# The beginning of a fused attention and feed-forward block: decay rows read back later, four x loads at once, values one chunk behind

## The chip, the core and the metric

The kernel runs on one core of one Trainium2 chip. The metric is the device time of one launch in microseconds (us), taken as the median of several runs.

## The reference

All tensors are float32. x has 8 batches of T = 1024 rows with V = 512 columns, D is 128, and there are three decays.

```python
xn = (x - mean(x)) / sqrt(var(x) + 1e-5)            # over the 512 columns
q, gate = xn @ Wq, softmax(xn @ Wg)                 # gate: 3 values a row
for i in range(3):
    k, v = xn @ Wk[i], xn @ Wv[i]
    decay = sigmoid(decay_logits[i])
    w[s, t] = decay ** max(t - s - 1, 0) * (t > s)  # used as in the reference's masked product
    blended += gate[..., i:i+1] * ((q @ k.T * w) @ v)
s = blended @ Wo * out_scale
g = silu(down(silu(gate_proj(xn)) * up(xn)))        # weights are lut[idx], 16 values, inner size 1376
out = x + s * g
```

Here `@` and the products over rows go batch by batch.

## The kernel before

The work is cut in two phases. `phase_1` takes each batch in 8 chunks of 128 rows, from chunk 7 down to chunk 0. In the generator `project`, a chunk is loaded (`load`, L289), its mean and variance are taken on VectorE (`statistics`, L297 to L301, with a power on GpSimd at L300), it is normalized in place (`normalize`, L312), transposed by four TensorE products with the identity and copied out of PSUM by ScalarE (`transpose`, L320 and L321), and multiplied by the value and gate weights (`values`, L327 and L330, tile `pv`). From the fifth chunk on each step also computes one of the four groups q, k0, k1, k2 for the upper half of the rows (`features`, L360 and L363, tile `pq`). For the first batch, b = 0, the statistics are on VectorE; for later batches they are on ScalarE (L304, L305).

`softmax` turns the gate logits of a half batch into gates: a maximum and a subtraction on VectorE (L338, L339), the exponential on ScalarE (L340), a sum, a reciprocal and a product (L343 to L345). The gates are then written to DRAM word by word, transposed (L347, tile `gTd`), and read back broadcast to all partitions (L351, tile `ga`). The generator `chunks`, which runs one batch behind `project`, multiplies `ga` by q (L425) and uses it in the scores (L450, tile `psc`), after it has transposed k (L441, tile `pk`).

`tables` prepares the decays. It loads three small inputs (L133 to L135), computes the decays, and fills `k_tab` and `c_tab` with powers on GpSimd (L149, L150). It writes `k_tab` to a DRAM scratch `pow_d` word by word (L152), and reads two overlapping windows of it back into the tiles `back` (L156). Two copies that reverse the rows (L163) make `w_tab` and `q_tab`. `more_weights` loads the gate and value weights (L92, L94), and in its second step the weights of q and k and `wo` (L98 to L103). `gate_up_weights` builds the feed-forward weights from the table of 16 values, with VectorE steps in `look_up` (L174 to L198) on index blocks `idx` loaded at L213 to L215.

`phase_2` does the feed-forward and the output. It isn't touched.

The order of work is written by hand: the loop of `phase_1` advances the generators `older` (chunks), `newer` (project), `setup` (tables) and `weights` (look-up) in turns, and `keep_order` pins TensorE, VectorE, ScalarE and GpSimd to the order in which the instructions were written. SyncE, which issues nearly all of phase 1's loads, is pinned to the written order only up to the start of that loop. The x tiles have four buffers (`xp`, `bufs=4`), and the PSUM tiles of `project` also four (`p_a`, tag "a"). Before the first chunk, nine products of the identity with itself keep TensorE working (L518). A DMA instruction on SyncE that has to wait holds up all that are behind it.

Of the kernel before, what the change touches and what calls it, by code (L numbers as in the profile page):

```python
# [10 lines left out]
F32 = mybir.dt.float32  # L11
# [7 lines left out]
P = 128  # L19
# [19 lines left out]
def recurrent_block(ctx: ExitStack, tc, x, wq, wk, wv, wo, wg, decay_logits, out_scale, lut, gidx, uidx, didx, out):  # L39
# [18 lines left out]
    nc = tc.nc  # L58
    B, T, V = x.shape
    D = wq.shape[1]  # L60
    NI = wk.shape[0]
# [3 lines left out]
    NC = T // P  # L65
# [23 lines left out]
    wo_sb = const.tile([P, V], F32)  # L89

    def more_weights(wvg_sb, wqk_sb):
        nc.sync.dma_start(out=wvg_sb[:, :, NI * D :], in_=wg.rearrange("(c p) d -> p c d", p=P))  # L92
        for i in range(NI):
            nc.sync.dma_start(  # L94
                out=wvg_sb[:, :, i * D : (i + 1) * D], in_=wv[i].rearrange("(c p) d -> p c d", p=P)
            )
        yield
        nc.sync.dma_start(out=wqk_sb[:, :, :D], in_=wq.rearrange("(c p) d -> p c d", p=P))  # L98
        for i in range(NI):
            nc.sync.dma_start(  # L100
                out=wqk_sb[:, :, (i + 1) * D : (i + 2) * D], in_=wk[i].rearrange("(c p) d -> p c d", p=P)
            )
        nc.sync.dma_start(out=wo_sb, in_=wo)  # L103
# [3 lines left out]
    ident = const.tile([P, P], F32)  # L107
# [20 lines left out]
    def tables():  # L128

        nc.sync.dma_start(out=dl, in_=decay_logits.partition_broadcast(P))  # L133
        nc.sync.dma_start(out=lut_sb, in_=lut.partition_broadcast(P))
        nc.sync.dma_start(out=osc, in_=out_scale.partition_broadcast(P))  # L135
        nc.gpsimd.iota(e_int, pattern=[[0, NI]], base=0, channel_multiplier=1)
        nc.gpsimd.memset(e_c, float(P))
        nc.gpsimd.memset(zero, 0.0)
        nc.sync.dma_start(out=pow_d[:, :P], in_=zero)
        yield  # L140

        nc.vector.tensor_scalar(dl, dl, -87.0, None, ALU.max)
        nc.scalar.activation(dec, dl, AF.Exp, scale=-1.0)
        nc.vector.tensor_copy(e_k, e_int)
        nc.vector.tensor_tensor(lut_x, lut_i[:, :, 0:1], lut_i[:, :, 1:2], ALU.bitwise_xor)
        yield
        nc.vector.tensor_scalar(dec, dec, 1.0, None, ALU.add)
        nc.vector.reciprocal(dec, dec)
        nc.gpsimd.tensor_tensor(k_tab, dec, e_k, ALU.pow)  # L149
        nc.gpsimd.tensor_tensor(c_tab, dec, e_c, ALU.pow)  # L150
        with nc.allow_non_contiguous_dma(reason="384 words, once"):
            nc.sync.dma_start(out=pow_d[:, P:].rearrange("i s -> s i"), in_=k_tab)  # L152
        backs = []
        for step, first in ((1, 0), (0, P)):
            back = small.tile([P, NI, P], F32, name="back", tag="back", bufs=2)
            nc.sync.dma_start(  # L156
                out=back, in_=bass.AP(pow_d.tensor, pow_d.offset + first, [[step, P], [2 * P, NI], [1, P]])
            )
            backs.append(back)
        for _ in range(4):  # L160
            yield
        for tab, back in zip((w_tab, q_tab), backs):
            nc.vector.tensor_copy(tab, back[:, :, ::-1])  # L163
            yield
# [102 lines left out]
            nc.sync.dma_start(out=wd_d[j], in_=t[:, : 7 * V // 2])  # L267


    def project(b, pools, sides, kept):  # L270


# [4 lines left out]
        wvg_sb, wqk_sb = sides  # L277
# [9 lines left out]
        def load(c):  # L287
            xts[c] = xp.tile([P, V], F32, name=f"x{b}_{c}", tag="x")
            nc.sync.dma_start(out=xts[c], in_=x[b, ts(c, P), :])  # L289
# [27 lines left out]
        def transpose(c):  # L317
            pt = p_a.tile([P, NV, P], F32, name=f"pt{b}_{c}", tag="a")
            for v in range(NV):
                nc.tensor.transpose(pt[:, v, :], xts[c][:, ts(v, P)], ident)  # L320
            nc.scalar.copy(xnT[:, :, ts(c, P)], pt)  # L321

        def values(c):

            pv = p_a.tile([P, NI * D + NI], F32, name=f"pv{b}_{c}", tag="a")
            for v in range(NV):
                nc.tensor.matmul(  # L327
                    pv, lhsT=xnT[:, v, ts(c, P)], rhs=wvg_sb[:, v, :], start=(v == 0), stop=(v == NV - 1)
                )
            nc.scalar.copy(v_sb[:, c, :], pv)  # L330
# [38 lines left out]
        yield  # L369
        if b == 0:  # L370
            load(NC - 2)
            statistics(NC - 1)
        load(NC - 3)
        normalize(NC - 1)
        statistics(NC - 2)
        yield
        for k in range(NC):
            c = NC - 1 - k
            transpose(c)
            if c > 0:  # L380
                normalize(c - 1)
            if c > 1:
                statistics(c - 2)
            if c > 2:
                load(c - 3)
            yield
            if k >= NC // 2:
                features(1, k - NC // 2)
            half = softmax(1) if k == NC // 2 else iter(())
            next(half, None)  # L390
            yield
            next(half, None)
            values(c)
            yield
        ts_ = tp.tile([P, 4, 2, U], F32, name=f"ts{b}", tag="ts")
        b11, b12, b21, b22 = (xnT[:, 2 * r : 2 * r + 2, ts(hf, U)] for r in (0, 1) for hf in (0, 1))
# [2 lines left out]
        for k in range(NC // 2):  # L399
# [3 lines left out]
            half = softmax(0) if k == 0 else iter(())  # L403
# [85 lines left out]
    def phase_1():  # L489
        nonlocal small, p_a, p_c, p_r  # L490
        with (
            tc.tile_pool(name="p_a", bufs=4, space=PSUM) as p_a,
            tc.tile_pool(name="p_c", bufs=3, space=PSUM) as p_c,
            tc.tile_pool(name="p_r", bufs=1, space=PSUM) as p_r,
            tc.tile_pool(name="xnp", bufs=2) as xnp,
            tc.tile_pool(name="tp", bufs=1) as tp,
            tc.tile_pool(name="xp", bufs=4) as xp,
            tc.tile_pool(name="wts", bufs=1) as wts,
            tc.tile_pool(name="build", bufs=1) as build,
            tc.tile_pool(name="wgup", bufs=1) as wgup,  # L500
            tc.tile_pool(name="att", bufs=2) as att,
            tc.tile_pool(name="chk", bufs=2) as chk,
            tc.tile_pool(name="blp", bufs=1) as blp,
            tc.tile_pool(name="pairp", bufs=1) as pairp,
            tc.tile_pool(name="small", bufs=3) as small,
        ):
            pools = (xp, xnp, tp, att)
            weights = chain(gate_up_weights(build, wgup, pairp), down_weights(build, wgup))
            wvg_sb = wts.tile([P, NV, NI * D + NI], F32, name="wvg_sb", tag="wvg_sb")
            wqk_sb = wts.tile([P, NV, (NI + 1) * D], F32, name="wqk_sb", tag="wqk_sb")  # L510

            def build_some(n):
                for _ in range(n):
                    next(weights, None)

            warm = p_a.tile([P, P], F32, name="warm", tag="a")
            for _ in range(9):
                nc.tensor.matmul(warm, lhsT=ident, rhs=ident, start=True, stop=True)  # L518
            kept = {}
            ending = iter(())  # L520
            newer = project(0, pools, (wvg_sb, wqk_sb), kept)
            setup = tables()
            more = more_weights(wvg_sb, wqk_sb)
            next(newer)
            next(more)
            next(newer)
            next(setup)
            next(more, None)
            keep_order(tc, seen, (mybir.EngineType.SP,))
            for b in range(B + 1):  # L530
                following = project(b + 1, pools, (wvg_sb, wqk_sb), kept) if b + 1 < B else iter(())
                older = chunks(b - 1, (chk, blp), kept) if b else iter(())
                for k in range(NC):
                    next(older, None)
                    next(newer, None)
                    next(setup, None)
                    busy = (b > 0 or k >= NC // 2) and b < B
                    build_some(1 + (0 < b < B))
                    if k < NC // 2:
                        for _ in range(2):  # L540
                            next(ending, None)
                    next(newer, None)
                    build_some(busy * (1 + (b > 0)))
                    next(older, None)
                    build_some(busy * 2)
                    if k < NC // 2:
                        next(ending, None)
                    if k >= NC - 2:
                        next(following, None)
                    next(newer, None)  # L550
                    next(older, None)
                for g in (older, ending):
                    for _ in g:
                        pass
                ending, newer = newer, following
            for _ in weights:
                pass
# [388 lines left out]
```

## Time and profile before

| | |
|---|---|
| median of three runs | 2192.69 us (2191.36 to 2192.97) |
| the profiled execution's own time | 2192.99 us |
| its span in the profile | 2190.8 us (2.2 us lie around it) |
| TensorE (PE) busy | 2170.4 us, 99% |
| VectorE (DVE) busy | 1114.2 us, 51% |
| ScalarE (ACT) busy | 829.8 us, 38% |
| GpSimd (POOL) busy | 916.7 us, 42% |
| mean granted clock of TensorE | 0.997 |

Times in the profile count from the start of the span. In a timeline a row has the start, the time of the merged group, engine, line, operation, output and inputs, and the number of instructions; in brackets stands the idle time of the engine before it and what ended that. SPq is the queue of SyncE, where a row is the issue of a DMA, not its transfer. The granted clock is 1.00 in most slices of the beginning, and 0.50 in the slices from 8 to 11 us and in part of those from 35 to 43 us. The share of the DMA engines in a slice can exceed 1.00 a little, because packets are counted in the slice in which they begin.

### The profile page before, as it was taken

How to read it: one execution, taken by the hardware profiler on the slowest of the kernel's cores; microseconds unless marked ns; L12 is line 12 of the kernel's file. 1: busy time of each engine (PE TensorE's matmuls, PEld its weight loads, DVE VectorE, ACT ScalarE, POOL GpSimd, SP SyncE). 2: the span in 40 equal slices, each digit the busy share in tenths (PEclk: the TensorE clock that was granted, in tenths of full speed). 3: DMA queues.
4: the chain of work that ended last, by engine and by line, in shares of the span. 5: the costliest groups of instructions: out<-in, count | busy, mean ns of one | idle time of the engine just before them, and what ended most of it. 6: DMA issues, size and time to landing. Idle time of an engine off the chain costs nothing.

```text
span 2190.8 us, 25235 instructions
## 1 busy us (share of the span) xinstructions
PE 2170.4 (99%) x9218; PEld 1598.1 (73%) x9218; DVE 1114.2 (51%) x1589; ACT 829.8 (38%) x1795; POOL 916.7 (42%) x800
## 2 busy tenths in 40 slices
PE   7999999999999999999999999999999999999998
PEld 4666666666668778678857876885787688578867
DVE  5887868688635435433533443353344335433533
ACT  2666666666434214312421431242144124313410
POOL 1535454334243553424525441453445153434512
PEclk9999999999999999999999999999999999999999
DMA  4785655435284434333532442343244234234501
GB/s 122 190 215 199 172 169 179 174 125 175 77 319 155 145 106 144 121 116 131 166 117 85 151 131 106 132 161 112 95 153 147 106 116 152 90 132 147 164 24 53
DMA packets 137153, 305.29 MB, mean 139 GB/s; under 512 B 50147, under 2 KB 71910, under 8 KB 136006
## 3 DMA queue, kind: packets, MB, share of 16 engines
q1 hardware_dynamic: 129302, 279.82, 39.1%
q0 software_dynamic: 7728, 23.86, 3.0%
q8 instruction: 73, 1.20, 0.2%
q14 instruction: 50, 0.41, 0.1%
HBM read 225.72 MB, written 77.93 MB: 139 GB/s over the span
## 4 chain that ended last, share of the span: by engine, by line
PE 95%; DMA 2%; POOL 1%; ACT 1%; issue 1%; DVE 0%; SPq 0%; POOLq 0%; DVEq 0%
PE s L663 27%; PE ds L807 22%; PE fs L617 9%; PE pq L360 9%; PE pv L327 7%; PE sE L663 4%; PE fsE L617 4%; PE po L472 3%; PE ds L818 2%; PE ps L829 2%; PE psc L450 2%; PE pu L458 1%; PE pt L320 1%; DMA x<-in_x 1%; PE pk L441 1%; DMA xs<-xsd 1%
## 5 line engine op out<-in xcount | busy, mean ns | idle before, releaser
L663 PE MATMUL s<-xs,wq 128*128 128x256 f32 x2688 | 602.9, 380 | 0.0
L663 PEld LDWEIGHTS s<-xs,wq 128*128 128x128 f32 x2688 | 508.7, 190 | 78.4 <-DVE sE L690 2.7
L807 PE MATMUL ds<-wd,s 128*128 128x256 f32 x1280 | 286.7, 379 | 0.0
L807 PEld LDWEIGHTS ds<-wd,s 128*128 128x128 f32 x1280 | 243.2, 190 | 33.0
L360 PE MATMUL pq<-xnT,wqk_sb 128*128 128x512 f32 x512 | 231.9, 596 | 0.0
L807 PE MATMUL ds<-wd,h 128*128 128x256 f32 x960 | 222.9, 379 | 0.0
L807 PEld LDWEIGHTS ds<-wd,h 128*128 128x128 f32 x960 | 182.3, 190 | 52.5 <-issue 27.0
L617 PE MATMUL fs<-xs,wr 128*128 128x512 f32 (+1 forms) x480 | 215.4, 592 | 0.0
L719 POOL TENSOR_TENSOR u<-u,e 128x512 f32<-128x512 f32 x64 | 79.9, 1270 | 276.0 <-DVE u L715 276.0
L327 PE MATMUL pv<-wvg_sb,xnT 128*128 128x387 f32 x512 | 179.6, 493 | 3.7 <-ACT xnT L321 2.4
L686 DVE TENSOR_TENSOR s<-s,e 128x512 f32<-128x512 f32 x112 | 78.3, 699 | 187.5 <-ACT s L685 187.5
L617 PEld LDWEIGHTS fs<-xs,wr 128*128 128x128 f32 (+1 forms) x480 | 86.8, 181 | 115.9 <-issue 112.4
L360 PEld LDWEIGHTS pq<-xnT,wqk_sb 128*128 128x128 f32 x512 | 93.0, 192 | 92.8 <-issue 92.8
L832 POOL TENSOR_TENSOR gx<-gx 128x512 f32<-128x512 f32 x63 | 80.3, 1274 | 184.7 <-DVE gx L830 141.2
L327 PEld LDWEIGHTS pv<-wvg_sb,xnT 128*128 128x128 f32 x512 | 93.4, 192 | 59.9 <-ACT xnT L321 4.8
L306 POOL TENSOR_SCALAR rstd<-rstd 128x1 f32<-128x1 f32 x56 | 27.5, 490 | 248.8 <-ACT junk L305 248.3
L601 POOL TENSOR_TENSOR xs<-xs 128x1792 f32<-128x1792 f32 (+1 forms) x38 | 127.9, 3383 | 7.4 <-issue 6.4
L690 DVE TENSOR_TENSOR sE<-s,e 128x512 f32<-128x512 f32 x112 | 78.3, 699 | 85.7 <-PE s L663 85.7
L848 ACT ACTIVATE gx<-ds 128x256 f32<-128x256 f32 x32 | 12.3, 384 | 287.1 <-PE ds L818 287.1
L663 PE MATMUL sE<-xs,wq 128*128 128x256 f32 x448 | 115.0, 379 | 0.0
L681 ACT COPY e<-sE 128x512 f32<-128x512 f32 x112 | 65.6, 586 | 123.7 <-PE sE L663 123.7
L723 POOL TENSOR_TENSOR h<-h,e 128x512 f32<-128x512 f32 x64 | 79.9, 1273 | 57.5 <-issue 46.4
(146 smaller groups left out, 3252.0 us busy)
## 6 DMA issues: line engine op xcount, KB each, us to landing
wq<-quadd SPq DMA_DIRECT2D x112, 896.0 KB, 4.5
xs<-xsd SPq DMA_DIRECT2D x8, 3584.0 KB, 11.8
x<-in_x SPq DMA_DIRECT2D x64, 256.0 KB, 5.5
xsd<-ts SPq DMA_DIRECT2D x8, 2048.0 KB, 8.7
gx<-in_x SPq DMA_DIRECT2D x64, 256.0 KB, 2.9
out<-gx POOLq DMA_DIRECT2D x63, 256.0 KB, 2.3
wr<-wgud SPq DMA_DIRECT2D x16, 896.0 KB, 4.6
ga<-gTd SPq DMA_DIRECT2D x16, 768.0 KB, 5.3
```

The costliest lines, as they stand in the source:

```text
L327: nc.tensor.matmul(pv, lhsT=xnT[:, v, ts(c, P)], rhs=wvg_sb[:, v, :], start=(v == 0), stop=(v == NV - 1))
L360: nc.tensor.matmul(pq, lhsT=wqk_sb[:, v, ts(j, D)], rhs=xnT[:, v, ts(hf, U)], start=(v == 0), stop=(v == NV - 1))
L472: nc.tensor.matmul(po, lhsT=lh, rhs=rh, start=(n == 0), stop=(n == len(prods) - 1))
L601: nc.gpsimd.tensor_tensor(o, x1, x2, ALU.subtract)
L617: nc.tensor.matmul(ps, lhsT=w[:, 2 * W_OF[k] + n, :m], rhs=xs[:, X_OF[k], 2 * n : 2 * n + 2, :], start=start and n == 0, stop=stop and n == 1,
L663: nc.tensor.matmul(self.t[n][:, ts(a, H)], lhsT=self.w[:, a, (0, 1, 6, 2, 3, 4, 5)[i - 1], :], rhs=self.xs[:, X_OF[self.k], D_OF[i], :], s ...
L686: nc.vector.tensor_tensor(self.t[1], self.t[1], self.e, ALU.add)
L690: nc.vector.tensor_tensor(self.t[3], self.t[2], self.e, ALU.add)
L719: nc.gpsimd.tensor_tensor(o[:, n], o[:, n], other[:, n], ALU.add)
L723: nc.gpsimd.tensor_tensor(of_h(half, n), of_h(half, n), two(other[:, n]), ALU.mult)
L807: nc.tensor.matmul(ps, lhsT=lhs[k][:, n, :], rhs=wd_sb[n][:, ts(D_OF[k], H)], start=start and n == 0, stop=stop and n == NK - 1, skip_grou ...
L832: (nc.vector if end else nc.gpsimd).tensor_tensor(g, g, xr, ALU.add)
```

## The change

The weights of the gates and values are loaded from ScalarE's queue. For the first batch four x chunks are loaded at once at the start; so the load of chunk 4 is no longer made in the loop. In `tables` three of the yields before the copies are moved ahead of the read back, so that the back reads are written three slots after the write, with two more slots before the copies. For the first batch `values` runs one chunk behind `transpose`, and the upper half's softmax one step later. The warm products become a helper: twelve at the start, and five more after the first chunk's transposes.

```diff
     def more_weights(wvg_sb, wqk_sb):
-        nc.sync.dma_start(out=wvg_sb[:, :, NI * D :], in_=wg.rearrange("(c p) d -> p c d", p=P))
+        nc.scalar.dma_start(out=wvg_sb[:, :, NI * D :], in_=wg.rearrange("(c p) d -> p c d", p=P))
         for i in range(NI):
-            nc.sync.dma_start(
+            nc.scalar.dma_start(
                 out=wvg_sb[:, :, i * D : (i + 1) * D], in_=wv[i].rearrange("(c p) d -> p c d", p=P)
             )
...
             nc.sync.dma_start(out=pow_d[:, P:].rearrange("i s -> s i"), in_=k_tab)
+        for _ in range(3):
+            yield
         backs = []
...
             backs.append(back)
-        for _ in range(4):
+        for _ in range(2):
             yield
...
+    def warm_up(n):
+
+        warm = p_a.tile([P, P], F32, name="warm", tag="a")
+        for _ in range(n):
+            nc.tensor.matmul(warm, lhsT=ident, rhs=ident, start=True, stop=True)
+
...
         if b == 0:
             load(NC - 2)
+        load(NC - 3)
+        if b == 0:
+            load(NC - 4)
             statistics(NC - 1)
-        load(NC - 3)
         normalize(NC - 1)
         statistics(NC - 2)
         yield
+        lag = 1 if b == 0 else 0
         for k in range(NC):
             c = NC - 1 - k
             transpose(c)
...
-            if c > 2:
+            if c > 2 and (b, k) != (0, 0):
                 load(c - 3)
+            if b == 0 and k == 0:
+                warm_up(5)
             yield
             if k >= NC // 2:
                 features(1, k - NC // 2)
-            half = softmax(1) if k == NC // 2 else iter(())
+            half = softmax(1) if k == NC // 2 + lag else iter(())
             next(half, None)
             yield
             next(half, None)
-            values(c)
+            if k >= lag:
+                values(c + lag)
+            if lag and k == NC - 1:
+                values(0)
             yield
...
-            warm = p_a.tile([P, P], F32, name="warm", tag="a")
-            for _ in range(9):
-                nc.tensor.matmul(warm, lhsT=ident, rhs=ident, start=True, stop=True)
+            warm_up(12)
```

## The prediction

> **What bounds the kernel now.** I began with the page's busy table: PE is busy for 2170.4 of 2190.8 us, so the end moves only if PE idles less, runs at a better clock or does less work. Next I asked for the waits of PE over the whole span, to see where the missing time lies.
>
> ```profile
> PE pt L320 <- DVE x L312: 7.9, 2, 7.0
> PE pv L327 <- ACT xnT L321: 2.4, 4, 0.7
> PE po L472 <- POOL qb L429: 1.4, 1, 1.4
> PE warm L518 <- POOL nhalf L110: 1.4, 1, 1.4
> PE pv L327 <- DMA wvg_sb<-in_wv: 1.3, 1, 1.3
> ```
>
> Columns: us in total, times, longest. Nearly all of it belongs to the first batch's beginning, one wait of 7.0 us above all. PE's timeline puts it in place:
>
> ```profile
> 28.14 2.77 PE L327 MATMUL pv<-wvg_sb,xnT 128*128 128x387 f32 x8
> 37.94 1.12 PE L320 MATMUL pt<-ident,x 128*128 128x128 f32 x4 [7.03 <-DVE x L312]
> 38.84 5.19 PE L360 MATMUL pq<-xnT,wqk_sb 128*128 128x512 f32 x8
> ...
> 60.20 3.60 PE L360 MATMUL pq<-xnT,wqk_sb 128*128 128x512 f32 x8
> 63.64 0.83 PE L450 MATMUL psc<-ga,kT 128*128 128x128 f32 x6
> ```
>
> After chunk 3 PE has nothing until 37.94, then works at half clock: 5.19 us for a group that takes 3.60 at 60.20. From here to the end PE loses under 3 us. So the whole change is worth what it does to the start of the first psc, 63.64 us, which lies one to one on the end. SyncE's timeline tells why chunk 2 was late:
>
> ```profile
> 17.68 0.38 SPq L152 DMA_DIRECT2D powd<-k_tab  x1
> 18.11 0.48 SPq L213 DMA_DIRECT2D idx<-in_gidx  x1
> ...
> 27.49 0.90 SPq L156 DMA_DIRECT2D back<-powd  x2
> 28.49 1.54 SPq L289 DMA_DIRECT2D x<-in_x  x3
> ...
> 43.22 0.38 SPq L347 DMA_DIRECT2D gTd<-g  x1
> ...
> 54.91 0.33 SPq L351 DMA_DIRECT2D ga<-gTd  x1
> ```
>
> The two back reads wait 9.8 us for the landing of k_tab's write, and the loads of x chunks 2, 1, 0 stand behind them. The gates use the same kind of write: 11.7 us from gTd's issue to ga's. DVE shows when ga lands, with 3.9 us to spare before psc:
>
> ```profile
> 59.76 0.56 DVE L425 TENSOR_TENSOR ga<-ga,qT 128x384 f32<-128x384 f32 x1 [2.03 <-DMA ga<-gTd]
> ```
>
> **Step by step.** The instruction orders of both kernels show what moves. Line numbers are those of before.
>
> *First microseconds.* Four x loads go out on SP, wg and three wv on ACT: four issue slots of about 0.5 us on each queue instead of eight in a row. ACT's table load (1.28 us) slips behind its four issues, to about 4 us; ACT's first copy is at 6.72, so that costs nothing, and 2 us of cover would remain. DMA engines were at 1.11, 1.10 and 0.87 of their share in the slices from 5 to 8 us, so no bandwidth appears: pv needs wv, at 7.97 before; with x4's 256 KB in between (0.7 us at 373 GB/s) I put it at 8.7 (bounds 7, wv first, to 10). The warm matmuls take 3.76 us for nine, so 12 end at 6.4, the transposes of chunk 7 at 6.8, five more at 8.9, chunk 6 at 9.3. pv of chunk 7 then runs to 11.9 at full clock (before: 7.97 to 12.3, 4.50 us, at 0.50 in the slices 8 to 11). Gain here 0.4.
>
> The Trainium skill (DMA: Bandwidth & Descriptors, "Issuing engines are not separate DMA queues") speaks against this edit: a second issuing queue saves only issue time. Those full slices agree, and the sum would be the same by either.
>
> *Chunk 5.* Its normalize stands on DVE behind the look-up (L174) that waits for the first idx; in before that began at 13.85. idx is issued about as early as before, so I take its landing at 13.4 (bounds 12 to 15). PE idles from 11.9 to about 14.5. The lag removes three waits of 0.68 us for ACT's copies; they fall ahead of this wait and the next, so I count nothing.
>
> *x3, x2.* SP's new order puts the second idx block (512 KB) ahead of wq, wk, wo, x3, x2. In before x3 landed 4.55 us after idx (13.85 to 18.40). 512 KB at the 300 GB/s of the slices 12 to 14 is 1.7 us: x3 lands at 19.7, x2 at 20.4 instead of 35.12. x3 to its transposes was 2.8 us (18.40 to 21.16), so they start at 22.5. One round of transpose, pq and pv is 6.48 us (46.48 to 52.96): chunk 2 at 29.0, chunk 1 could begin at 35.5. The 7.03 us wait and the half clock behind it are gone.
>
> *The write and what is behind it now.* k_tab itself is ready 3.8 us after idx (13.85 to 17.65), so near 17.3; but its write stands on the queue behind x3 and x2, whose data occupy the DMA engines to about 19.9. In before its data moved 0.9 us after the issue at 17.68, and the landing came 8.9 us after that. So it lands at 28.8 (bounds 27.0, nothing ahead, to 31). Then SP issues one back read, x1, the other back, x0. x1 is 2.8 us (first x: 0.74 to 3.57), 0.5 for back's issue and about 0.5 for its 192 KB: 32.5 (bounds 30.8 to 35.5). Call this L.
>
> *From x1 to the gates.* DVE meets, in order: statistics of x1 1.06 (37.80 to 38.86), four look-up steps 3.5 (0.72, 0.84, 1.20, 0.71), normalize x1 0.46, statistics of x0 1.07, a leaf 0.72, red and g 0.3, two COPY_PREDICATED 2.56 and a leaf 0.72, then sm and the product 0.6: 10.95 us. In before red came right after the statistics, 4.5 us after x2's landing. So gTd is issued at 43.45, not earlier than 43.22. 11.69 us to ga's issue, 4.85 to DVE, 0.6 for the product: psc starts at L + 28.1 = 60.6.
>
> *PE on that path.* Chunk 1 transposes at L + 5.05 = 37.55 (2 us idle after 35.5). Then three groups of transposes, pq 13.8, three more pv and pk are 19.8: ready for psc at 57.3, idle 3.3 us until 60.6. psc moves from 63.64 to 60.6: 3.0 less.
>
> *Clock.* 3.3 us of idle: the row at 8 to 11 us (0.50 after only 0.66 us of work between 5.1 and 7.97) says it can halve the clock, at 1.6 us (4.50 against 2.87); an idle gap cut in two by a period of the gate would cost nothing. Bounds 0 and 1.7, taken 0.8, half.
>
> The Trainium skill (TensorE: Matmul & The Clock Gate, "What you observe" and what follows it) has a free-running window of about 3.4 us and asks for a wholly idle one. The row above had work in its window and still lost the clock, so row and rule differ; by the rule this term would be 0.
>
> Sum: -3.0 + 0.8 = -2.2. The profiled execution took 2192.99 us, so 2190.8; that is 0.3 above the median, and from the median 2192.69 it is **2190.5**. With L and the clock at their ends: -4.8 to +1.6 (L = 30.8 without clock; 35.5 with), 2187.9 to 2194.3. My bound for a difference is 0.2%, 4.4 us.
>
> **Rivals.** *The path to psc is shorter* (faster). If the write drains faster, or x1 slips in earlier, PE's own work becomes the bound: chunk 1 at 35.5 plus 19.8 is 55.3, 8.4 less: 2184.3. For it: 8.9 us from moved data to landing is for 384 words, and the second idx block, read in the same stretch at 27 GB/s (22 to 28), may have held it up; nothing is queued behind it now. Against: gates with 1536 words took 11.7 with the engines nearly empty. It decides if L falls below 31.2; typical 2186.5.
>
> *The early queue jams* (slower). Small loads (dl, lut, osc) now wait for wg and wv on reused lanes, and the second idx block is ahead of the weights. If idx lands at 20 instead of 13.4, look-up, k_tab, x3 and gates all shift: L reaches 39.1, psc 67.2, 3.6 later, and with clock loss at both gaps (3.3) the time is 2199.6. It decides from L = 40 alone, or 36.6 with those losses. For it: dl, lut and osc already land 5 to 6 us after issue. Against: SP reissues from 6 us on in before, too, and the look-up began at 13.85.
>
> *The stall only moves.* If gTd comes at its old time plus what L slips, psc stays at 63.6 and nothing changes: L = 35.5. It is inside the forecast's range.
>
> **Chances.** Forecast 0.50 (it and the moved stall, both within 0.2%), shorter path 0.36, jam 0.14. I give the shorter path much because L's two largest terms, 8.9 and 3.7, come from one event each. The range runs from 2185.5, leaving out a tenth at the faster end, to 2196.0; the jam is mostly outside.
>
> **What would show it.** Right: no 7 us wait at chunk 2; SP's two back issues split by an x load; psc idle on ga with gTd near 43; half clock at that gap or not. First pv near 9.3. k_tab's landing near 28.8, x1 near 32.5. Wrong: gTd clearly before 42 (shorter path), idx after 16 (jam), or a wait of more than 1 us after 66 us that before does not have, which no step of mine foresees.

## The result, and the profile after

| | before | after |
|---|---|---|
| median of eight runs | 2192.82 us (2191.36 to 2193.44) | 2198.91 us (2197.02 to 2201.52) |
| ratio to before | | 1.0029, 95% interval 1.0018 to 1.0040 |
| the profiled execution, its span | 2192.99 us, 2190.8 | 2197.51 us, 2195.7 |
| TensorE (PE) busy | 2170.4 us | 2171.0 us |

The change made the kernel 6.1 us slower, where I had predicted 2.2 us faster. The profiled execution of after is one of its quicker ones; its span is 4.9 us longer, and PE is busy for only 0.6 us more. So PE idles more. The longest of its waits over the whole span, in the columns us in total, times, longest:

```profile
PE pv L335 <- ACT xnT L329: 7.4, 1, 7.4
PE pt L328 <- DVE x L320: 4.8, 4, 2.1
PE psc L466 <- DVE ga L441: 2.8, 1, 2.8
```

The 7.0 us at chunk 2 are gone, and a single wait of 7.4 us stands in another place: a `pv` that waits for ScalarE's copy of `xnT`. PE's timeline of after says where:

```profile
35.33 0.63 PE L328 MATMUL pt<-ident,x 128*128 128x128 f32 x4 [0.31 <-DVE x L320]
...
51.68 3.60 PE L368 MATMUL pq<-xnT,wqk_sb 128*128 128x512 f32 x8
58.12 0.94 PE L466 MATMUL psc<-ga,kT 128*128 128x128 f32 x6 [2.84 <-DVE ga L441]
...
115.41 0.83 PE L466 MATMUL psc<-ga,kT 128*128 128x128 f32 x6
123.67 5.05 PE L335 MATMUL pv<-wvg_sb,xnT 128*128 128x387 f32 x8 [7.43 <-ACT xnT L329]
```

The first psc starts at 58.12 us, 5.5 earlier than in before. More than that is lost at 123.67, far behind, in the second batch, whose code the change does not touch. The same `pv` in before:

```profile
121.08 2.88 PE L327 MATMUL pv<-wvg_sb,xnT 128*128 128x387 f32 x8 [0.37 <-ACT xnT L321]
```

There it waits 0.37 us and takes 2.88 us; in after it waits 7.43 and takes 5.05, because the granted clock was 0.50 from 121.3 to 128.1 us. The account of the two spans: -5.5 for the start of psc, +0.7 for a wait of the product `po` on its input `pr` at 63.00, +7.1 for the wait (7.43 less 0.37), +2.2 for the half clock, +0.3 for a wait at 627 us: +4.8, against 4.9 measured. Two stretches of both kernels, first of before, then of after, show the same (length, busy PE, PEld, DVE, ACT, POOL, each with its instructions, then granted clock, share of the DMA engines, GB/s):

```profile
66.00:132.00 66.00, 65.63 (x322) 44.40 (x321) 54.94 (x59) 41.28 (x110) 36.53 (x33) 1.00 0.79 176
132.00:2190.00 2058.00, 2051.34 (x8727) 1522.91 (x8725) 1021.27 (x1449) 768.33 (x1640) 865.76 (x739) 1.00 0.41 138
```

```profile
66.00:132.00 66.00, 58.56 (x279) 39.50 (x279) 48.71 (x52) 37.39 (x101) 32.61 (x30) 0.95 0.75 167
132.00:2190.00 2058.00, 2056.04 (x8744) 1525.57 (x8742) 1021.08 (x1449) 769.81 (x1643) 862.10 (x737) 1.00 0.41 137
```

From 66 to 132 us PE is busy for 7 us less and at a lower clock. Behind 132 us the waits are alike: up to its last product PE idles 1.8 us in before and 2.0 us in after. The 4.7 us of busy time by which the second rows differ are the end, since the last product ends at 2185.16 us in before and at 2190.07 in after.

**What the copy waited for.** ScalarE works in the order written. Its timeline in after, and then the same row of before:

```profile
118.25 0.63 ACT L312 ACTIVATE junk<-x 128x512 bf16<-128x512 f32 x1 [11.79 <-DMA x<-in_x]
...
123.02 0.60 ACT L329 COPY xnT<-pt 128x512 f32<-128x512 f32 x1
```

```profile
115.66 0.63 ACT L304 ACTIVATE junk<-x 128x512 bf16<-128x512 f32 x1 [4.65 <-DMA x<-in_x]
```

The statistics of x chunk 0 of batch 1 (the last chunk of that batch) wait for its load, and the copy of `xnT` stands ten rows behind them on the engine. SyncE's queue shows that load, L297 of after at 104.32, L289 of before at 108.88:

```profile
103.69 0.51 SPq L245 DMA_DIRECT2D quadd<-pair  x1
104.32 0.58 SPq L297 DMA_DIRECT2D x<-in_x  x1
105.42 0.62 SPq L355 DMA_DIRECT2D gTd<-g  x1
```

```profile
108.25 0.51 SPq L243 DMA_DIRECT2D quadd<-pair  x1
108.88 0.58 SPq L289 DMA_DIRECT2D x<-in_x  x1
109.56 1.03 SPq L347 DMA_DIRECT2D gTd<-g  x1
```

The order is the same: a write of feed-forward weights (`pair`, 896 rows of 2 KB, 1.8 MB), the x load, the gates' 1536 words. But the load lands 13.9 us after its issue in after (118.22) and 6.75 in before (115.63). The trace has 16 increments of the semaphore of this load: in after 15 lie between 111.04 and 111.15, and the last is at 118.22. In before all lie between 115.45 and 115.63. So one share of 16 was late. In after the words start at 109.95 us and the gates' write lands at 120.59, and the late share came while they drained. How slow the queue is meanwhile, its other packets show: a 2 KB packet took 0.10 us on average in the four us ahead of the first word, and 0.61 us from 2 to 8 us behind it (in before 0.10 and 0.77). And one thing is seen at just that time: an 8 KB packet on an instruction queue (q14 of the page) at 110.26 us, which took 0.32 us. In before such packets lie at 101.67 and 125.84, away from the load. The other instruction queue (q8) has none near it, the nearest in after being at 91.62 and 127.32.

The Trainium skill (DMA: Bandwidth & Descriptors, "Why a DMA increments its semaphore by 16 and not by 1") says that a transfer is spread over up to 16 DMA engines, that each adds its own part to the semaphore, and that only the full 16 means that all has landed. The 15 that came 7 us ahead of the last agree.

### The profile page after: what moved, and what is told of

It is laid out like the page before. It is cut to its first block, busy times and chain, and to the rows that moved or that the text cites. A ratio compares the mean times of both kernels' runs of the same rounds, so it can differ in the third digit from the quotient of the medians.

```text
span 2195.7 us, 25271 instructions
## 1 busy us (share of the span) xinstructions
PE 2171.0 (99%) x9234; PEld 1599.3 (73%) x9234; DVE 1111.9 (51%) x1589; ACT 830.0 (38%) x1795; POOL 912.6 (42%) x800
## 4 chain that ended last, share of the span: by engine, by line
PE 94%; DMA 3%; DVE 1%; POOL 1%; issue 1%; ACT 1%; ACTq 0%; SPq 0%; POOLq 0%; DVEq 0%
PE s L677 27%; PE ds L821 22%; PE fs L631 9%; PE pq L368 8%; PE pv L335 6%; PE sE L677 4%; PE fsE L631 4%; PE po L488 3%; PE ds L832 2%; PE ps L843 2%; PE psc L466 2%; PE pu L474 1%; PE pt L328 1%; DMA x<-in_x 1%; PE pk L457 1%; DMA xs<-xsd 1%
## 5 line engine op out<-in xcount | busy, mean ns | idle before, releaser
L862 ACT ACTIVATE gx<-ds 128x256 f32<-128x256 f32 x32 | 12.3, 384 | 287.1 <-PE ds L832 287.1
```

## The experiments

Theory A: the x load is caught in the word write because one DMA engine is late, and (its finer form) what makes it late is the fetch of instructions, which moves when the four weight loads leave SyncE's program. Its rival B differs from run to run and stands in each expectation. The times of before beside these runs had medians from 2193.06 to 2193.16 us.

**1. The load on another queue.** After, with

```diff
+            queue = nc.scalar if (b, c) == (1, 0) else nc.sync
-            nc.sync.dma_start(out=xts[c], in_=x[b, ts(c, P), :])
+            queue.dma_start(out=xts[c], in_=x[b, ts(c, P), :])
```

> The changed kernel, but the last x chunk of the second batch (chunk 0, b = 1) is loaded from ScalarE's queue instead of SyncE's; in the changed kernel it stands on SyncE behind the 896 KB write of a weight pair and just ahead of the gates' word write. Theory A (one DMA engine of 16 was late with this load, and its part was caught behind the word write's drain, 7 us): the load lands before the words start, the 7.4 us wait of pv and the half clock behind it (2.3 us) are gone, about 9.3 us less than the changed kernel: near 2189, that is some 4 us faster than before. Rival B (the DMA engines as a whole are full there, and an earlier beginning brings the user of the load nearer): the load is late from any queue, and the time stays within 2 us of the changed kernel's, 2197 to 2201.

Measured: 2188.97 us (2187.88 to 2190.78), ratio 0.9983 (0.9973 to 0.9992). PE has no wait at that `pv`. ScalarE issues the load ahead of the pair write, and it lands at 100.98:

```profile
98.27 0.35 ACTq L298 DMA_DIRECT2D x<-in_x  x1
```

The next x load on SyncE, chunk 7 of batch 2, took its place between pair and words, and it was caught instead: 15 shares by 112.29, the last at 120.75. Nobody needed it yet. The medians of the two kernels lie 9.9 us apart, and the wait and the half clock made 9.3 in the account above: what after lost hangs on this load. (The pair write is 1.8 MB; the 896 KB of the expectation are its 896 rows misread.) The first psc stood at 58.47 behind 2.84 us of idle, with half clock from 59.7 to 63.1.

**2. The fetch moved.** After, with four one-word writes on SyncE in the first batch, so that its program is as long as before up to there:

```diff
+    idle_d = [dram.tile([1, 1], F32, name=f"idled{n}", tag=f"idled{n}") for n in range(4)]
...
+        for t in idle_d if b == 0 else ():
+            nc.sync.dma_start(out=t, in_=xnT[:1, 0, :1])
```

> The changed kernel with four extra one-word DMA writes on SyncE after the first batch's transposes, into scratch that nothing reads. They move no data to speak of, but shift what SyncE has behind it by four instructions, among it the moments at which its instruction memory is refilled by an 8 KB read on the DMA engines. Theory A with its finer form (the late engine is late because such an 8 KB instruction read came upon it at 110.3 us): the read falls elsewhere, the load lands with the other 15 engines, about 9 us less than the changed kernel, near 2189. Theory A without that cause, and rival B: as the changed kernel, 2197 to 2201, or up to 1 us more.

Measured: 2189.73 us (2188.46 to 2190.94), ratio 0.9984 (0.9974 to 0.9993). The fetch lies at 97.05 us, 6.8 ahead of the pair write; the x load's shares land by 111.17 (15) and 111.42 (last); the wait at `pv` is 0.52 us. Four transfers of one word took 9 us off the kernel, with queue and order of the load unchanged.

**3. The weights back on SyncE.** After, with the four weight loads on `nc.sync`, as in before.

> The changed kernel with the value and gate weights loaded from SyncE again; all else as in the changed kernel. The first pv then waits for wv a little longer (within 2 us), which the later wait for x3 hides. Theory A in its finer form: SyncE has its four instructions back, the instruction read falls elsewhere, no caught load: near 2189. Theory A without it, and rival B: 2197 to 2201.

Measured: 2189.95 us (2188.29 to 2191.28), ratio 0.9986 (0.9976 to 0.9995). Fetch at 96.26, all shares by 110.39, and the wait at `pv` is 0.29 us. The words start at 109.25 here, as early as in after, and the load stays on SyncE: an earlier beginning alone does not make it late. Without this part of the change after is 9.0 us faster; the rest of it is worth 3.1 us against before.

**4. Before, with only the weights on ScalarE** (the first four lines of the diff and nothing else).

> The kernel before with one part of the change alone: the value and gate weights are loaded from ScalarE. The beginning should stay about as before (the reads back still stand ahead of x chunks 2, 1 and 0). Theory A in its finer form: SyncE has four instructions fewer, as in the changed kernel, the instruction read meets the load of the second batch's last chunk, and about 7 to 9 us are lost: 2199 to 2202. Rival B (only an earlier beginning makes the load late): as before, 2191 to 2194.

Measured: 2195.62 us (2193.68 to 2198.20), ratio 1.0012 (1.0003 to 1.0021). Neither number holds, since I had not foreseen that this edit changes the beginning, too:

```profile
58.51 0.83 PE L450 MATMUL psc<-ga,kT 128*128 128x128 f32 x6
...
120.93 5.07 PE L327 MATMUL pv<-wvg_sb,xnT 128*128 128x387 f32 x8 [5.35 <-ACT xnT L321]
```

With the four loads gone, SyncE's order puts the second index block ahead of the weights of q and k, the 7 us wait at chunk 2 shrinks to 0.44, and psc starts 5.1 us earlier. Then the load is caught (fetch at 109.78, 15 shares by 110.50, the last at 115.48). -5.13 for psc, +4.98 for the wait and +2.19 for the half clock make +2.0; the spans differ by 1.7. This one edit brings a beginning nearly as good as after's, and the loss with it.

The Trainium skill (DMA: Bandwidth & Descriptors, "Issuing engines are not separate DMA queues") lets a second issuing queue save issue time only. It says nothing of what the move does to the first queue, and here that was the larger part: the order of SyncE's queue changed and psc came 5.1 us earlier, and a later load was caught, which cost 7.2 us of wait and half clock.

**5 and 6. The gates first.** The 2.84 us that psc waits go back to DVE's look-up steps ahead of the gates' softmax. The loop of `phase_1` holds them back in two of the first batch's slots and makes them up in the next two:

```diff
+                    held = b == 0 and k in (NC // 2, NC // 2 + 1)
+                    caught = b == 0 and k > NC // 2 + 1
-                    build_some(1 + (0 < b < B))
+                    build_some((1 + (0 < b < B)) * (1 - held + caught))
...
-                    build_some(busy * (1 + (b > 0)))
+                    build_some(busy * (1 + (b > 0)) * (1 - held + caught))
...
-                    build_some(busy * 2)
+                    build_some(busy * 2 * (1 - held + caught))
```

Number 5 is number 1 with this edit:

> As the run with the second batch's last x chunk on ScalarE's queue, and with the first batch's look-up steps of the fifth and sixth slots moved to the seventh and eighth, so that on VectorE the gates' softmax no longer stands behind four look-up steps and two COPY_PREDICATED. Theory C (after the change the gates' word write is what ends last before the first psc): gTd is issued near 36 instead of 41.4, ga is there before PE wants it, the 2.84 us wait and the half clock after it in that run's profile (3.4 us at half, some 1.7 us) go: 2184.5 to 2186.5. Rival D (VectorE only delays its own later work by as much, and PE waits there): 2188 to 2190, with a new wait of PE on VectorE after 58 us.

Measured: 2185.30 us (2183.73 to 2186.27), ratio 0.9963 (0.9950 to 0.9976), the best version: 7.8 us faster than before and 13.6 faster than after. The gates are issued at 36.03 (41.02 in after), and psc follows pq with no wait, as theory C had it. Chunk 7 of batch 2 was caught here as in number 1 (15 shares by 108.95, the last at 117.49, the fetch at 108.02), again at no cost to PE:

```profile
53.42 3.60 PE L369 MATMUL pq<-xnT,wqk_sb 128*128 128x512 f32 x8
56.86 0.83 PE L467 MATMUL psc<-ga,kT 128*128 128x128 f32 x6
```

Number 6 is number 3 with this edit:

> As the run with the weights on SyncE again, and with the same look-up steps held back. There PE waited 1.5 us for ga and 1.7 us for pr behind it. Theory C: both go, 2186.5 to 2188.5. Rival D: 2189 to 2191. If the shifted SyncE order catches another load behind a word write, a wait of pv on xnT of 5 to 7 us shows it, at whatever time.

Measured: 2186.41 us (2185.38 to 2186.83), ratio 0.9969 (0.9958 to 0.9981). psc is at 54.09 without a wait, but the 1.73 us that a `po` waits for `pr` at 60.04 stayed, against what I expected.

**7. Before, with only the back reads later** (three yields ahead of them, two instead of four behind).

> The kernel before with one part of the change alone: the decay rows are read back three slots later. SyncE then has x chunk 2 ahead of the back reads, but behind k_tab's write and the second idx block; x1 and x0 stay behind the back reads. If only SyncE's wait for the landing held x2 up: x2 lands near 23, the 7 us wait and the half clock go, 2186 to 2189. If the word write's drain holds every transfer behind it, as for the caught load: x2 lands at 28 to 31, and 2188 to 2191 at best; x1 no earlier than 33.

Measured: 2190.09 us (2187.64 to 2190.98), ratio 0.9985 (0.9976 to 0.9995).

```profile
17.75 0.38 SPq L152 DMA_DIRECT2D powd<-k_tab  x1
...
19.83 0.40 SPq L291 DMA_DIRECT2D x<-in_x  x1
27.19 0.90 SPq L158 DMA_DIRECT2D back<-powd  x2
```

```profile
34.66 1.12 PE L322 MATMUL pt<-ident,x 128*128 128x128 f32 x4 [4.39 <-DVE x L314]
```

The load of x chunk 2 is now issued at 19.83 and not behind the back reads, but it lands at 31.82: it is queued behind `k_tab`'s 384 words and the second index block, and waits for them in the engines instead of on SyncE (the words land at 27.12, the block at 31.16). It is held up like the caught load, in the first 32 us. psc starts 2.7 us earlier.

**8. Before, with only the values and the softmax one chunk later.**

> The kernel before with one part of the change alone: in the first batch values one chunk behind the transposes, and the upper half's softmax a step later. By the prediction's step this part gains nothing by itself, and the gates come later (the softmax stands behind x0's statistics and three look-up steps): 2192 to 2196. If SyncE's order, which is not pinned here, moves x2 ahead of the back reads as a side effect, x2 is there 4 to 12 us earlier and the time falls to 2188 to 2192.

Measured: 2194.43 us (2193.93 to 2194.93), ratio 1.0006 (0.9997 to 1.0016), which can't be told from no change. Here, too, SyncE's order moved: x chunk 2 went ahead of the index block (18.53), and its wait fell to 3.72 us. But the gates went out 3.4 us later (46.67), and what was won stands ahead of psc:

```profile
63.77 1.65 PE L454 MATMUL psc<-ga,kT 128*128 128x128 f32 x6 [2.83 <-DVE ga L429]
```

**9. A fetch moved into the load, first try.** Before, with the tables' four small transfers (L133 to L135, L139) on `nc.scalar`, which shortens SyncE's program by four, as number 4 does.

> The kernel before with four other SyncE transfers of the first microseconds (the three small inputs of the tables and the zero rows) issued by ScalarE; SyncE's order from 40 us on is that of before, four instructions earlier in its program, as in the kernel with only the weights moved. If the instruction fetch is the cause (A): an 8 KB fetch that lay at 101.67 us, ahead of the pair write, now comes behind that write's issue, near 110 us; x chunk 0 of batch 1 is caught in the gates' word write, lands 11 to 14 us after its issue instead of 6.75, and PE waits 4 to 8 us for xnT near 121 us, with half clock there. Time: 2193 plus the shift of the first psc against 63.64 plus 6 to 9 us. If the fetch is a coincidence and the earlier start or the weights' queue is the cause (B): that wait stays under 1 us and the time is 2193 plus the shift of the first psc, within 1.5 us.

Measured: 2192.11 us (2191.35 to 2193.95), ratio 0.9994 (0.9985 to 1.0004), as B had it. The wait at `pv` is 0.54 us. But the fetch came at 114.62, when 15 of the load's shares had landed (114.38 to 114.54); the last came at 114.72. So the premise of A was not met, and the run does not decide between the two. It shows that a shorter program alone is not enough, and no more.

**10. Two small writes instead of four** (number 2 with `range(2)`).

> The changed kernel with two one-word writes on SyncE instead of the four of the second experiment. If the fetch is the cause (A): it comes two SyncE instructions earlier than 110.26 us, that is 104 to 107 us, while the pair write's data still move. An engine that is late then is still late when the words come, so x chunk 0 of batch 1 is still caught: a wait of 3 to 8 us at that pv and 2196 to 2201 us; only if the engine makes up its delay before the words start does the wait go, 2189 to 2191 us. If the two extra semaphore turns of the queue, and not the fetch, were what helped in the second experiment (B), the wait shrinks by about half, with the fetch where it will, 2193 to 2196 us.

Measured: 2192.32 us, but from 2189.37 to 2197.93 in ten runs, more than three times the spread of number 2; ratio 1.0001 (0.9991 to 1.0010). In the profiled execution (2189.90 us) the fetch is at 107.32, 3.2 us behind the pair write; the shares lie apart, from 111.33 to 112.04, and none is caught. The median lies between what A had for the two outcomes and just under B's range. The spread is what one expects where an engine's delay is at times made up before the words come and at times not; the executions without a profile do not show it.

**11. One late engine, made on purpose.** Before, with one row of 14 KB behind the pair write and ahead of the x load:

```diff
+    late_d = dram.tile([1, 28 * P], F32, name="lated", tag="lated")
...
                 nc.sync.dma_start(out=to[:, :, 3:7, :], in_=pair)
+                if o == 1:
+                    nc.sync.dma_start(out=late_d, in_=pair[:1].rearrange("p k t m -> p (k t m)"))
```

> The kernel before with one more SyncE transfer behind the first pair write and ahead of the load of x chunk 0 of batch 1: one row of 14 KB from one partition to a scratch row, which occupies one DMA engine for about half a microsecond (an 8 KB packet took 0.31 us). The beginning is as in before. If one engine that is late is enough (A): 15 of the 16 shares of the x load land together, near 115.6 us, and the last only after the gates' words have drained, 4 to 8 us later; PE waits 4 to 8 us for xnT near 121 us, and the time is 2197 to 2202 us, or scatters between 2193 and 2202 if the margin is as narrow as with two small writes. If the lateness of one engine isn't what costs (B): all shares land within 0.6 us, the wait stays under 1 us, and the time is 2192 to 2194 us.

Measured: 2199.99 us (2198.34 to 2201.80), ratio 1.0031 (1.0019 to 1.0042). SyncE's queue and PE's timeline:

```profile
108.99 0.51 SPq L244 DMA_DIRECT2D quadd<-pair  x1
109.55 0.50 SPq L246 DMA_DIRECT2D lated<-pair  x1
110.17 0.35 SPq L292 DMA_DIRECT2D x<-in_x  x1
110.63 1.19 SPq L350 DMA_DIRECT2D gTd<-g  x1
```

```profile
126.21 5.53 PE L330 MATMUL pv<-wvg_sb,xnT 128*128 128x387 f32 x8 [4.75 <-ACT xnT L324]
```

Fifteen shares of the x load land by 116.37, the last at 120.77. PE waits 4.75 us and then runs at half clock. The fetch stays at 102.45, out of the way. In the profile psc is 0.7 us later than in before; the wait is worth 4.4 us more and the half clock 2.7, 7.8 in all, and the spans differ by 8.0. One transfer of 14 KB that no other work needs costs 6.8 us in the medians: a delay of one share is enough.

The runs side by side (us; the load is the x load between pair and words, in numbers 1 and 5 another chunk's):

| kernel | pair issued | words start | fetch | 15 shares by | 16th share | wait at pv |
|---|---|---|---|---|---|---|
| before | 108.25 | 114.50 | 101.67 | 115.63 | 115.63 | 0.37 |
| after | 103.69 | 109.95 | 110.26 | 111.15 | 118.22 | 7.43 |
| 1 | 104.78 | 111.04 | 111.36 | 112.29 | 120.75 | none |
| 2 | 103.80 | 110.06 | 97.05 | 111.17 | 111.42 | 0.52 |
| 3 | 103.00 | 109.25 | 96.26 | 110.36 | 110.39 | 0.29 |
| 4 | 103.04 | 109.30 | 109.78 | 110.50 | 115.48 | 5.35 |
| 5 | 101.45 | 107.71 | 108.02 | 108.95 | 117.49 | none |
| 6 | 101.31 | 107.56 | 94.34 | 108.67 | 108.70 | 0.35 |
| 7 | 105.51 | 111.77 | 98.89 | 112.89 | 112.91 | 0.37 |
| 8 | 110.07 | 116.32 | 102.59 | 117.44 | 117.45 | 0.34 |
| 9 | 107.17 | 113.42 | 114.62 | 114.54 | 114.72 | 0.54 |
| 10 | 104.11 | 110.37 | 107.32 | 111.72 | 112.04 | 0.92 |
| 11 | 108.99 | 115.27 | 102.45 | 116.37 | 120.77 | 4.75 |

Without the made delay of number 11, the load is caught in four runs, and in these the fetch begins 0.3 to 0.5 us behind the first word. In all the others it is more than a microsecond from it, and the load is not caught. Numbers 3 and 6 have the words as early as after or earlier, so the early beginning is not what costs.

## Why the prediction was wrong

**The step that failed** is in its first part: "From here to the end PE loses under 3 us. So the whole change is worth what it does to the start of the first psc, 63.64 us, which lies one to one on the end." The first sentence was true of before; the second took it over to after. The start of psc moved by 5.5 us, in the direction foreseen, and more than that was given back at 123.67: what the sum put at nothing was 9.3 us there (7.1 of wait, 2.2 of half clock). It came with the move of the four weight loads, since after without this part has no such wait (experiment 3) and before with this part alone has it (experiment 4). Experiments 1 and 2 take that one loss away and leave 4.1 and 3.4 us of gain. The prediction named this as what would make it wrong (a wait of more than 1 us after 66 us), but gave it no price and no chance. None of its rivals held it: the jam was to come from a late index block, and that landed early.

What the profile of before could have told: the load of x chunk 0 of batch 1 sits between a write of 1.8 MB (896 rows of 2 KB) and a word write of 15.8 us (109.56 to 125.40), and DVE and ScalarE work in order, so any further delay of it meets PE. ScalarE already waited 4.65 us for that load in before, and PE 0.37. That this margin would be lost could not be read from it; that it was that thin could.

**First microseconds:** pv first at 8.79 (9.3 predicted). Right; ACT's slipped table load cost nothing.

**Chunk 5, x3, x2:** the index block landed at 12.3 (13.4), x3 at 18.94 (19.7), x2 at 19.62 (20.4). Right in kind: the 7.03 us wait is gone. What I did not see is that more than one edit does it: the move of the weights is enough (experiment 4), and so is the rest of the change without it (experiment 3, whose first psc is at 56.36).

**The write of k_tab** was mis-sized: 28.8 predicted, 24.65 measured, 8.4 us after its issue at 16.24. My lower bound, with nothing ahead, had been 27.0. Its words moved behind the loads, as foreseen (half of them by 18.82), but landed 5.8 us after that; the sum had 8.9 for this, and in before it is 8.7 on the same count. Why they drained faster stays open: the index block queued behind them, which the rival blamed, is there in experiment 3, too, and there it was 6.4. From the landing to L the sum had 3.7 us and it took 5.4, because x1, issued at 25.14, landed only at 30.06. So L was 30.1, not 32.5, and the two errors cancelled in part, by luck.

```profile
16.24 0.38 SPq L152 DMA_DIRECT2D powd<-k_tab  x1
24.66 0.38 SPq L158 DMA_DIRECT2D back<-powd  x1
25.14 0.43 SPq L297 DMA_DIRECT2D x<-in_x  x1
...
41.02 0.38 SPq L355 DMA_DIRECT2D gTd<-g  x1
...
51.70 0.33 SPq L359 DMA_DIRECT2D ga<-gTd  x1
```

**From x1 to the gates, and PE on that path:** with the measured L both sums hold. gTd at L + 10.95 is 41.05 (41.02), psc at L + 28.1 is 58.2 (58.12), chunk 1's transposes at L + 5.05 are 35.15 (35.33). The wait of psc was 2.84 us (3.3). The split of 11.69 for the words and 4.85 to DVE was 10.68 and 5.45:

```profile
57.15 0.92 DVE L441 TENSOR_TENSOR ga<-ga,qT 128x384 f32<-128x384 f32 x1 [7.39 <-DMA ga<-gTd]
```

**Clock:** taken at 0.8, halfway. In the profiled run of after the 2.84 us of idle cost no clock; in experiment 1 the same 2.84 cost 3.4 us of half clock. Both ends occurred, and the traces say why. In all thirteen the clock changes only on a grid of 3.413 us. Of the windows of this grid at full clock, all 16 in which PE idled for 2.09 us or more were followed by one at half clock, and none in which it idled for 1.90 us or less. In after the grid cut the idle time at 56.43 into 1.14 and 1.69 us, in experiment 1 at 56.29 into 0.66 and 2.18. That a cut gap costs nothing was in the prediction; where the cut falls was chance.

**The shorter path** was what the beginning did (L under 31.2), but PE's own work did not become the bound, as that rival had it: psc still waited for ga. Without the loss it is 2189 to 2190 us in experiments 1 to 3, not the rival's 2184.3 or its typical 2186.5; to reach that, the gates had to go ahead of the look-up (5 and 6).

## What to carry to other kernels

In these runs a write of single words held back the transfers queued right behind it and those caught beside it, so look in the profile for the loads that stand next to one, and count how much each of them may slip before an engine that works in order stops. A load that is needed soon belongs on another queue or well ahead of such a write, not in between. After any edit that adds or drops instructions on a queue, read the waits of the whole span, since the place of an unrelated loss can be far from the edit.

## What the runs showed of the hardware

- In before and after `k_tab`'s 384 words took 9.8 and 8.4 us from issue to landing, the gates' 1536 words 8.4 to 15.8. Transfers queued behind them or caught beside them came late by as much: x chunk 2 in experiment 7 took 12.0 us, the late sixteenth of a load came 7.1 us behind the others, and the x load issued behind the gates at 110.70 in before landed at 125.58, when they did (125.40).
- One share out of 16 that is late by less than a microsecond seems enough, if words come next: the pair write in after had 15 increments by 110.56 and the last at 111.44. The margin is narrow: in experiment 4 the last was 0.16 us behind and the x load was caught, in experiment 9 it was 0.14 behind and the load was not.
- Fetches of instructions stand in the trace as DMA packets of 8 KB on a queue of their own. Four more instructions in SyncE's program moved one by 13 us (110.26 to 97.05).
- The TensorE clock changed on a grid of 3.413 us, and about 2 us of idle time within one window (between 1.90 and 2.09) halved it for the next.
- A row of one partition, 14 KB, had its last increment at 116.27, 6.7 us after its issue: it landed together with the 15 punctual shares of the x load behind it (116.22 to 116.37), and the sixteenth did not come until 120.77.

**What stays open.** The records don't name the DMA engine of a packet, so that the fetch and the late share were on the same engine is inferred from times: a fetch 0.3 to 0.5 us behind the first word in the four caught cases, farther off in the others, and the made delay of experiment 11. That experiment shows that one late share is enough; that in after it was the fetch that made the share late is argued from experiments 2 and 3 and these times. Why after's own runs spread over 4.5 us, and why the last share came at 118.22 there and at 115.48 in experiment 4, wasn't settled.
